# First image's sampling in turn with the other images' offsets, with TensorE and VectorE in a written order

## The chip, the cores and the metric

The program runs on one core of one Trainium2 chip. The metric is the device time of one execution in microseconds (us); lower is better. A program computes on five engines: TensorE (PE, matrix products; the loading of weights into it is shown apart as PEld), VectorE (DVE), ScalarE (ACT), GpSimd (POOL) and SyncE (SP). Each works through its own queue of instructions in order and waits on semaphores where it needs another's result. Transfers between the chip's main memory and its on-chip buffers are issued from the queues of SP, ACT or POOL and run on 16 DMA engines. Results of PE land in PSUM, a small memory of banks, from where VectorE or ScalarE must fetch them.

## The reference

Four images of 64 x 64 pixels with 256 channels go through a deformable convolution block, then through additive attention and a feed-forward layer that treats half of the tokens. Everything is in 32-bit floats. The change touches the first block alone, cut here to what matters:

```python
xp = x @ in_w + in_b                                   # projection, padded to 66 x 66
x1 = silu(bn(depthwise_conv3x3(x)))                    # x is group-normalised before
offset = x1 @ off_w + off_b                            # 8 groups x 9 taps x 2
mask = softmax((x1 @ mask_w + mask_b).reshape(N, H, W, G, P), -1)
...
loc = ref + grid * OFFSET_SCALE + offset * (OFFSET_SCALE / norm)
samples = _bilinear_sample(img, 2.0 * loc - 1.0)       # per group and tap, at moved positions
out = (samples * m).sum(-1)
...
return out @ out_w + out_b                             # x = x + this
```

Each output pixel is, for each of 8 groups of channels, a weighted sum of bilinear samples at nine moved positions. While an offset stays within one pixel, all samples of a pixel lie in a 5 x 5 window around it. The kernel therefore makes 25 weights per pixel and group and sums 25 shifted products; the few tokens with larger offsets are gathered exactly.

## The kernel before

Tokens of an image (4096) are taken in slabs. The first stage, `offsets_and_weights` (L263), goes through all four images before anything else. It works in slabs of `SLAB` = 8 rows of 128 tokens, so four slabs an image, with these inner functions:

- `front` (L322) loads the image in eight pieces `xt` (SP's queue, pool `a_ld` with three buffers), turns them on PE (L339), takes `bn_stats` on VectorE (L341), copies them to `xn` on ScalarE (L342), and normalises at the end (L349 to L366). It is a generator; the next image's pieces are fetched two per slab.
- `convolution` (L412) is the depthwise 3 x 3: half of the channels as nine matmuls with diagonal weights per 512 tokens (L420), the other half as nine VectorE instructions per slab (L432, L434); SiLU on ScalarE.
- `taps` (L437) makes offsets and masks with PE (L444), VectorE adds the bias into `raw` (L448), and the softmax begins (L456 to L458).
- `window` (L461) ends the softmax (L463 to L465), stores `raw`, makes three `hat` weights on ScalarE (L473 to L477), and builds the 5 x 5 weights `w5` with three `my` (L483), nine `mxy` (L486) and nine additions (L488) on VectorE. Then PE turns `w5` (L497), ScalarE copies it to `wT` and SP stores it in `wt`.
- `projection` (L380) computes `xp` for 16 rows of pixels with PE (L387), stores it, and turns it in nine pieces (L405), which ScalarE copies to `tb` (L406) and SP stores in the table `tab` that the exact gathers read (L407).

In this stage the order of the instructions on each engine is chosen by the scheduler of the tile framework. PSUM is split into four buffers for turns (`a_t`) and four for matmuls (`a_m`).

Between the stages, borders of `xp` and `tab` are filled with zeros (L1387 to L1397, SP's queue).

The second stage is `sample_image(0, 6)` (L668), a generator of some 440 steps (`STEPS`). It lists the tokens that need exact rows (`list_tokens`, L534), then goes over four blocks of 1024 tokens, two halves of channels and 25 window positions. A step is one product of the shifted image `xs` with a weight `wb` (L697), or one addition into `ac` (L705). `wb` is a 512 KB load, spread over partitions (L688). The argument `depth` = 6 gives `wb` twelve buffers and `xs`, `prd` and `ac` two. Between the steps `exact_rows` (L563) gathers the listed tokens' samples on POOL's queue (L626) and sums them on VectorE (L637, L640). At the end of a block the output matmuls follow (L721), POOL adds the bias to the input rows `xr` (L725), VectorE adds both (L728) and SP stores the rows (L729).

After that, image by image, come attention preparation, attention and feed-forward. The sampling of images 1 to 3 runs as steps within these later stages, with `depth` = 1, so with two `wb` buffers.

`keep` marks an instruction as staying in the written order relative to the other marked ones of its engine; `Pinned` (L254) wraps VectorE so that all its operations are marked.

Of the kernel before, what the change touches and what calls it, by code (L numbers as in the profile page):

```python
# [45 lines left out]
def layers_kernel(ctx: ExitStack, tc: tile.TileContext, a, out: bass.AP):  # L46
# [207 lines left out]
    class Pinned:  # L254


        def __getattr__(self, name):
            op = getattr(nc.vector, name)
            return lambda *args, **kw: keep(op(*args, **kw))  # L259

    pinned = Pinned()

    def offsets_and_weights(images, slab, rows_bufs):  # L263

        ca = S.a_one
# [52 lines left out]
        diag = ca.tile([P, K2, P], F32, name="diag")  # L318
        for tap in range(K2):
            nc.vector.tensor_scalar(diag[:, tap], ident, dwk[:, 1, tap : tap + 1], None, ALU.mult)  # L320

        def front(n):  # L322
# [8 lines left out]
            for s in range(8):  # L331
                xt = S.a_ld.tile([P, 4, C], F32, tag="xt", name="xt")
                nc.sync.dma_start(
                    out=xt, in_=x_d[n, s * 512 : (s + 1) * 512].rearrange("(t p) c -> p t c", p=P)
                )
                for k in range(CC):
                    pt = S.a_t.tile([P, 4, P], F32, tag="pt", name="pt")
                    for t in range(4):
                        nc.tensor.transpose(pt[:, t, :], xt[:, t, k * P : (k + 1) * P], ident)  # L339
                    ptf = pt.rearrange("p t q -> p (t q)")  # L340
                    nc.vector.bn_stats(st[:, k, s, :], ptf)  # L341
# [3 lines left out]
                    )  # L345
                yield
            mv = S.a_sm.tile([P, CC, 2], F32, tag="mv", name="mv")
            for k in range(CC):
                nc.vector.bn_aggr(mv[:, k, :], st[:, k].rearrange("p s f -> p (s f)"))  # L349
# [3 lines left out]
            nc.tensor.matmul(pg, gavgf, mv[:, :, 0], start=True, stop=True)  # L353
            gm = S.a_sm.tile([P, CC], F32, tag="gm", name="gm")
            nc.vector.tensor_copy(gm, pg)
            gv = S.a_sm.tile([P, CC], F32, tag="gv", name="gv")
            nc.vector.tensor_sub(gv, mv[:, :, 0], gm)
            nc.vector.tensor_mul(gv, gv, gv)
            nc.vector.tensor_add(gv, gv, mv[:, :, 1])
            pg2 = S.a_t.tile([P, CC], F32, tag="pt", name="pg2")  # L360
            nc.tensor.matmul(pg2, gavgf, gv, start=True, stop=True)
            gr = inv_std(S.a_sm, pg2, CC, "gr")
            nc.vector.scalar_tensor_tensor(gm, gm, -1.0, gr, ALU.mult, ALU.mult)
# [9 lines left out]
        for at, n in enumerate(images):  # L373
            xn = xns.pop(n)
            after = front(images[at + 1]) if at + 1 < len(images) else iter(())
# [4 lines left out]
            def projection(s):  # L380
                xp = xps[s % len(xps)]
                for h in range(2):
                    for f in range(CC):
                        pm = S.a_m.tile([P, 8, W], F32, tag="pm", name="pm")
                        r0 = 16 * s + 8 * h
                        for k in range(CC):
                            nc.tensor.matmul(  # L387
# [9 lines left out]
                for f in range(CC):  # L397
                    nc.sync.dma_start(out=xp_d[n][f][:, q0 : q0 + 16 * MP], in_=xp[:, f, : 16 * MP])
                for o in range(0, 16 * MP, P):
# [3 lines left out]
                    for c in range(2):  # L403
                        for f in range(CC):
                            nc.tensor.transpose(pt[:m, c, f, :], xp[:, f, o + c : o + c + m], ident)  # L405
                        nc.scalar.copy(tb[:m, :, :, c, :], pt[:m, c].rearrange("p f (e g) -> p f g e", g=GH))  # L406
                    nc.sync.dma_start(out=tabw[q0 + o : q0 + o + m], in_=tb[:m].rearrange("p f g c e -> p (f g c e)"))  # L407


            x1s, raws = {}, {}  # L410

            def convolution(s):  # L412
# [3 lines left out]
                for o in range(0, slab * P, 512):  # L416
                    pc = S.a_m.tile([P, 8, W], F32, tag="pm", name="pc")
                    for tap in range(K2):
                        r = r0 + o // W + tap // 3
                        nc.tensor.matmul(  # L420
                            pc, diag[:, tap], xn[:, 1, r : r + 8, tap % 3 : tap % 3 + W],
                            start=(tap == 0), stop=(tap == K2 - 1),
                        )
                    nc.scalar.activation(
                        x1[:, 1, o : o + 512], pc.rearrange("p r w -> p (r w)"), AF.Silu,
                        bias=bnsh[:, 1:2], scale=bns[:, 1:2],
                    )
                acc = x1[:, 0].rearrange("p (r w) -> p r w", w=W)
                for tap in range(K2):
                    src = xn[:, 0, r0 + tap // 3 : r0 + tap // 3 + 2 * slab, tap % 3 : tap % 3 + W]  # L430
                    if tap == 0:
# [73 lines left out]
            for s in range(ns):  # L505
                if s + 1 < ns:
                    convolution(s + 1)
# [970 lines left out]
```

## Time and profile before

| | |
|---|---|
| runs | 10553.36, 10569.91, 10557.95 us; median 10557.95 us |
| profiled execution | 10563.61 us, its span from first to last instruction 10561.9 us |
| mean granted TensorE clock | 0.917 |
| busy over the span | PE 9008.4 us (85%), VectorE 8547.2 (81%), ScalarE 7377.6 (70%), GpSimd 5265.2 (50%) |
| offsets of images 0, 1, 2, 3 | 190, 195, 196, 209 us, from 55 us on |
| sampling of image 0 | 845 to 1490 us |
| attention and feed-forward | 1490 us to the end |

The span is what the profiler sees of one execution; the time of a run has a little more around it. A line of a group names source line, engine, operation, written and read tiles, shape and count, then busy time and mean duration, then how long the engine stood idle just before these instructions and who ended that. A line of the timeline gives start, duration and, in square brackets, the idle time before. Durations of VectorE instructions that follow each other overlap by some 0.1 us, so the sum of durations is a little more than the busy time. A 32-bit matmul is recorded as two passes, so counts of matmuls are twice those in the source; transposes are one.

### The profile page before, as it was taken

The numbers are of one execution on the slowest core, as the hardware profiler recorded it, in microseconds if no ns is written. First come the engines' busy times: TensorE is split into PE (matmuls) and PEld (weight loads), VectorE is DVE, ScalarE is ACT, GpSimd is POOL, SyncE is SP. The second block draws the span as 40 slices with busy tenths as digits, with TensorE's granted clock in tenths as the row PEclk, the third lists the DMA queues.
The fourth block names the chain that finished last, engine by engine and source line by source line (L and its number), as shares of the span: only waits on it lengthen the run. The fifth ranks groups of instructions, "written<-read, shape, count | busy, mean of one in ns | idle before, by whom it ended". The sixth has DMA issues, their size and how long they took to land. (4 is left out here: it accounts for less than half of the span.)

```text
span 10561.9 us, 115936 instructions
## 1 busy us (share of the span) xinstructions
PE 9008.4 (85%) x38460; PEld 4375.8 (41%) x38460; DVE 8547.2 (81%) x13406; ACT 7377.6 (70%) x8389; POOL 5265.2 (50%) x3059
## 2 busy tenths in 40 slices
PE   7882029999999678999999589999999699999995
PEld 4551014444444343444444344444444344444443
DVE  7776879898989778989899679899898357777772
ACT  4450018888888528888888438888888379999991
POOL 0004307676555326767655327676555155555552
PEclk8985569999999889999999789999999799999997
DMA  3336752222222252212111352222111300000002
GB/s 119 107 138 180 206 167 70 61 67 64 70 64 73 98 167 60 52 55 58 51 55 50 116 152 53 53 54 54 52 59 41 101 13 9 10 8 7 7 5 75
DMA packets 381330, 766.00 MB, mean 73 GB/s; under 512 B 49105, under 2 KB 212593, under 8 KB 380689
## 3 DMA queue, kind: packets, MB, share of 16 engines
q1 hardware_dynamic: 324432, 678.78, 20.3%
q0 software_dynamic: 30144, 45.87, 2.9%
q10 hardware_dynamic: 26112, 33.56, 0.9%
q8 instruction: 309, 5.06, 0.2%
q14 instruction: 333, 2.72, 0.1%
HBM read 580.88 MB, written 177.14 MB: 72 GB/s over the span
## 5 line engine op out<-in xcount | busy, mean ns | idle before, releaser
L909 DVE TENSOR_TENSOR r<-nn,r 128x512 f32<-128x512 f32 x6144 | 3943.0, 683 | 861.5 <-PE nn L904 805.9
L904 PE MATMUL nn<-qn,kf 32*128 32x512 f32 (+1 forms) x12288 | 4518.8, 640 | 132.7 <-DVE r L909 95.8
L994 POOL TENSOR_TENSOR r<-r 128x1024 f32<-128x1024 f32 x1024 | 2708.8, 2645 | 2645.4 <-DVE r L909 2625.3
L988 ACT ACTIVATE r<-d 128x1024 f32<-128x1024 f32 x3072 | 3117.2, 1015 | 1085.4 <-DVE r L998 699.9
L894 PE MATMUL d<-qf,kf 32*128 32x512 f32 (+1 forms) x12288 | 3338.1, 632 | 76.5 <-DMA qf<-qf 43.1
L990 ACT ACTIVATE r<-r 128x1024 f32<-128x1024 f32 x3072 | 3124.1, 1051 | 32.6
L904 PEld LDWEIGHTS nn<-qn,kf 32*128 32x128 f32 (+1 forms) x12288 | 1399.4, 185 | 1902.1 <-DVE r L909 1450.5
L932 PE MATMUL pv<-v,et 128*128 128x257 f32 x8192 | 2105.3, 400 | 15.0 <-DVE acv L956 15.0
L932 PEld LDWEIGHTS pv<-v,et 128*128 128x128 f32 x8192 | 1507.6, 194 | 975.5 <-issue 768.6
L894 PEld LDWEIGHTS d<-qf,kf 32*128 32x128 f32 (+1 forms) x12288 | 1018.0, 186 | 1340.3 <-issue 736.1
L996 POOL TENSOR_TENSOR r<-r 128x512 f32<-128x512 f32 x1024 | 1335.8, 1304 | 92.7 <-DVE r L909 17.1
L705 DVE TENSOR_TENSOR ac<-ac,prd 128x1024 f32<-128x1024 f32 x768 | 991.8, 1291 | 8.8
L697 DVE TENSOR_TENSOR prd<-xs,wb 128x1024 f32<-128x1024 f32 x768 | 977.7, 1273 | 15.2 <-DMA wb<-wt 12.0
L626 POOL DMA_INDIRECT ga<-tab,tii x576 | 718.3, 1247 | 207.3 <-issue 117.7
L916 ACT ACTIVATE et<-et,nshift 128x512 f32<-128x512 f32 x1024 | 723.8, 707 | 28.2 <-DVE et L1001 28.2
L998 DVE TENSOR_TENSOR r<-r 128x512 f32<-128x512 f32 x1024 | 723.6, 707 | 4.1 <-POOL r L994 3.7
L1001 DVE TENSOR_TENSOR et<-r 128x512 f32<-128x512 f32 x1024 | 698.1, 682 | 0.4
L115 ACT ACT_TABLE_LOAD x9 | 11.5, 1283 | 799.3 <-DVE mv L259 703.0
L721 PE MATMUL pmo<-outwp,ac 128*128 128x256 f32 x512 | 135.7, 416 | 469.1 <-DVE ac L705 431.2
L480 POOL MEMSET w<- 128x1600 f32 x16 | 22.9, 1432 | 675.0 <-PE ptw L497 352.3
L721 PEld LDWEIGHTS pmo<-outwp,ac 128*128 128x128 f32 x512 | 100.8, 205 | 521.4 <-DVE ac L705 304.5
L420 PE MATMUL pc<-xn,diag 128*128 128x512 f32 x576 | 262.2, 609 | 33.4 <-ACT xn L366 33.4
(344 smaller groups left out, 5282.7 us busy)
## 6 DMA issues: line engine op xcount, KB each, us to landing
wb<-wt SPq DMA_DIRECT2D x800, 512.0 KB
tab<-tb SPq DMA_DIRECT2D x128, 256.0 KB
v<-t SPq DMA_DIRECT2D x64, 512.0 KB
xs<-xp SPq DMA_DIRECT2D x32, 680.0 KB
xp<-xp SPq DMA_DIRECT2D x32, 544.0 KB
xt<-in_x_dram SPq DMA_DIRECT2D x32, 512.0 KB
xr<-in_x_dram SPq DMA_DIRECT2D x64, 256.0 KB
t<-xr SPq DMA_DIRECT2D x64, 256.0 KB
```

Source lines behind the costliest of these rows:

```text
L697: keep(nc.vector.tensor_tensor(pr.rearrange("p (r w) -> p r w", w=W), src, wb.rearrange("p (r w) -> p r w", w=W), ALU.mult,))
L705: keep(nc.vector.tensor_add(ac[:, f, :], ac[:, f, :], pr))
L894: keep(nc.tensor.matmul(d[:, j, :], kf[g, blk, rows(kt)], qs[q][0][g, blk, :], start=True, stop=True))
L904: keep(nc.tensor.matmul(nn, kf[g, blk, rows(kt)], qs[q][1][g, blk, :], start=True, stop=True))
L909: keep(nc.vector.tensor_tensor(r[:, j, :], ns[j], r[:, j, :], ALU.mult))
L916: keep(nc.scalar.activation(ets[b], ets[b], AF.Exp, bias=nshift))
L932: keep(nc.tensor.matmul(pv, ets[b0 + i][:, rows(j)], v[:, k0 + i, :], start=(i == 0), stop=(i == PVB - 1)))
L988: keep(nc.scalar.activation(rs[b, p], ds.pop((b, p)), AF.Ln))
L990: keep(nc.scalar.activation(rs[b, p], rs[b, p], AF.Exp, scale=-1.0))
L994: keep(nc.gpsimd.tensor_tensor(rs[b, 1], rs[b, 1], rs[b, 2], ALU.add))
L996: keep(nc.gpsimd.tensor_tensor(rs[b, 1][:, 0], rs[b, 1][:, 0], rs[b, 3][:, 0], ALU.add))
L998: keep(nc.vector.tensor_add(rs[b, 1][:, 1], rs[b, 1][:, 1], rs[b, 3][:, 1]))
```

## The change

The first image's offsets stay a stage of their own. From the second image on, offsets and sampling of image 0 take turns, in an order written in the source: `offsets_and_weights` becomes a generator with five stops per slab, and the caller takes 4, 4, 4, 3 and 3 sampling steps at these stops. The slab is halved (`SLAB // 2`, eight slabs an image). All operations of TensorE and VectorE in this stage are marked by `keep`. The turning of `w5` becomes `turn`, one slab after its `window`; `convolution` is one slab ahead. In images 1 to 3 both halves of the channels of the depthwise convolution go to TensorE. Loads of `xt` move from SP's queue to POOL's, and stores of `xp`, `tab` and `wt` and the zero fill from SP's to ACT's; the zero fill moves ahead of the stage. Buffers: `a_ld` two instead of three, `wb` two instead of twelve, `xs` and `prd` one instead of two, `my` and `mxy` one instead of two, one `xps` instead of two, PSUM three `a_t`, three `a_m` and two for sampling.

```diff
-    pinned = Pinned()
+    pinned = Pinned(nc.vector)
...
+        vec, pe = pinned, Pinned(nc.tensor)
...
-        diag = ca.tile([P, K2, P], F32, name="diag")
-        for tap in range(K2):
-            nc.vector.tensor_scalar(diag[:, tap], ident, dwk[:, 1, tap : tap + 1], None, ALU.mult)
+        diag = ca.tile([P, CC, K2, P], F32, name="diag")
+        for k in (1, 0):
+            for tap in range(K2):
+                nc.vector.tensor_scalar(diag[:, k, tap], ident, dwk[:, k, tap : tap + 1], None, ALU.mult)
...
-                nc.sync.dma_start(
+                nc.gpsimd.dma_start(
                     out=xt, in_=x_d[n, s * 512 : (s + 1) * 512].rearrange("(t p) c -> p t c", p=P)
                 )
...
-                    nc.vector.bn_stats(st[:, k, s, :], ptf)
...
+                    ptfs.append(ptf)
+                yield
+                for k in range(CC):
+                    vec.bn_stats(st[:, k, s, :], ptfs[k])
                 yield
...
-                    nc.sync.dma_start(out=xp_d[n][f][:, q0 : q0 + 16 * MP], in_=xp[:, f, : 16 * MP])
+                    nc.scalar.dma_start(out=xp_d[n][f][:, q0 : q0 + 16 * MP], in_=xp[:, f, : 16 * MP])
...
+                for k in range(CC):
+                    if k == 0 and not at:
+                        acc = x1[:, 0].rearrange("p (r w) -> p r w", w=W)
...
+                        continue
+                    for o in range(0, slab * P, 512):
+                        pc = S.a_m.tile([P, 8, W], F32, tag="pm", name="pc")
+                        for tap in range(K2):
+                            r = r0 + o // W + tap // 3
+                            pe.matmul(
+                                pc, diag[:, k, tap], xn[:, k, r : r + 8, tap % 3 : tap % 3 + W],
+                                start=(tap == 0), stop=(tap == K2 - 1),
+                            )
...
+                vec.tensor_reduce(omax[:, n, s * slab : (s + 1) * slab], hat[:, 1], AX.X, ALU.max)
+                yield
...
                 for ey in range(3):
-                    my = S.a_w1p.tile([P, slab, GP], F32, tag="my", name="my", bufs=2)
+                    my = S.a_w1p.tile([P, slab, GP], F32, tag="my", name="my")
...
+                    yield
+
+            def turn(s):
...
-                        nc.sync.dma_start(out=wt_d[n][f, :, o : o + 512], in_=wT[: GH * ND])
-
-            ns = NT // slab
-            convolution(0)
-            for s in range(ns):
-                if s + 1 < ns:
-                    convolution(s + 1)
-                taps(s)
-                window(s)
-                for i in range(s * (H // 16) // ns, (s + 1) * (H // 16) // ns):
-                    projection(i)
-                for _ in range(8 // ns):
+                        nc.scalar.dma_start(out=wt_d[n][f, :, o : o + 512], in_=wT[: GH * ND])
...
+        for i in range(len(images) * ns):
+            at, s = divmod(i, ns)
+            if s == 0:
+                cur = ahead
+                after = front(images[at + 1]) if at + 1 < len(images) else iter(())
+            cur.taps(s)
+            if last:
+                last[0].turn(last[1])
+            last = cur, s
+            if s + 1 < ns:
+                cur.convolution(s + 1)
+            elif at + 1 < len(images):
+                ahead = image(at + 1)
+                ahead.convolution(0)
+            window = cur.window(s)
+            for part in range(4):
+
+                if part == 0 and s >= ns // 2 or part == 2 and s >= ns // 2 or s < ns // 2:
                     next(after, None)
-            for _ in after:
-                pass
+                if at:
+                    yield
+                next(window, None)
+            if at:
+                yield
+            for j in range(s * (H // 16) // ns, (s + 1) * (H // 16) // ns):
+                cur.projection(j)
+            if at == 0 and s == ns - 1:
+                yield
+        last[0].turn(last[1])
...
-    def sample_image(n, depth=1):
+    def sample_image(n, sums=1):
...
-            ac = S.dn.tile([P, CC, CH], F32, tag="ac", name="ac", bufs=min(depth, 2))
+            ac = S.dn.tile([P, CC, CH], F32, tag="ac", name="ac", bufs=sums)
...
-                    wb = S.dn.tile([P, CH], F32, tag="wb", name="wb", bufs=2 * depth)
+                    wb = S.dn.tile([P, CH], F32, tag="wb", name="wb", bufs=2)
...
-    with scope(
-        ("a_one", 1, 0), ("a_xn", 2, 0), ("a_ld", 3, 0), ("a_wk", 2, 0), ("a_w1p", 1, 0), ("a_sm", 2, 0),
-        ("a_t", 4, 1), ("a_m", 4, 1),
-    ):
-        offsets_and_weights(range(NB), SLAB, 2)
...
-    with scope(("smp", 2, 0), ("two", 2, 0), ("sb", 2, 0), ("dn", 1, 0), ("ps_m", 2, 1)):
-        for _ in sample_image(0, 6):
+    with scope(
+        ("a_one", 1, 0), ("a_xn", 2, 0), ("a_ld", 2, 0), ("a_wk", 2, 0), ("a_w1p", 1, 0), ("a_sm", 2, 0),
+        ("smp", 2, 0), ("two", 2, 0), ("sb", 2, 0), ("dn", 1, 0), ("a_t", 3, 1), ("a_m", 3, 1), ("ps_m", 2, 1),
+    ):
+        others = offsets_and_weights(range(NB), SLAB // 2, 1)
+        next(others)
+        first = sample_image(0, 2)
+        for at, _ in enumerate(others):
+            for _ in range((4, 4, 4, 3, 3)[at % 5]):
+                next(first, None)
+        for _ in first:
             pass
```

## The prediction

> **What bounds the kernel now.** I read first the busy tenths in 40 slices, to see which stages the change touches. The first six slices (264 us each) are the offsets of all images (a), then the sampling of image 0 (b); from the sixth on the attention runs, which the change does not touch.
>
> ```profile
> span 10561.9 us, 115936 instructions
> PE   7882029999999678999999589999999699999995
> DVE  7776879898989778989899679899898357777772
> PEclk8985569999999889999999789999999799999997
> DMA  3336752222222252212111352222111300000002
> ```
>
> Then the busy time by stretch, cut at the start of each image and at the end of sampling (columns: stretch, length, busy PE, PEld, DVE, ACT, POOL with counts, granted clock, DMA share, GB/s).
>
> ```profile
> 0.00:55.00 55.00, 17.11 (x80) 13.94 (x80) 39.31 (x138) 15.91 (x22) 18.77 (x52) 0.91 0.42 127
> 55.00:245.00 190.00, 158.23 (x612) 95.45 (x612) 138.36 (x184) 93.28 (x163) 6.79 (x12) 0.90 0.37 129
> ...
> 845.00:1490.00 645.00, 60.98 (x202) 48.57 (x202) 524.60 (x526) 0.00 (x0) 206.53 (x164) 0.53 0.65 193
> ```
>
> Stages a and b end one after the other at 1490 us, 14% of the span. An image costs 190 to 209 us, and neither engine is full: PE 158, VectorE 138, each stopping for the other. Sampling is VectorE alone: 525 of 645 us, with PE nearly idle at clock 0.53. Over the 1490 us VectorE is busy 1118. So 372 us are VectorE's idle time, and that is all that interleaving can win, apart from work taken off it.
>
> Third, the groups of the two stages (before 845, and 845 to 1500):
>
> ```profile
> L434 DVE SCALAR_TENSOR_TENSOR x<-xn,dwk,x 128x1024 f32<-128x1024 f32 x128 | 163.4, 1277 | 2.7
> L488 DVE TENSOR_TENSOR w<-w,mxy 128x576 f32<-128x576 f32 x144 | 108.3, 752 | 0.5
> L448 DVE TENSOR_TENSOR raw<-po,omb 128x432 f32<-128x432 f32 x64 | 37.7, 603 | 95.8 <-PE po L444 95.8
> L406 ACT COPY tb<-ptc 128x256 f32<-128x256 f32 (+1 forms) x288 | 98.1, 385 | 53.2 <-PE ptc L405 28.5 <-DMA tab<-tb 24.0
> ...
> L637 DVE TENSOR_TENSOR ga<-ga,wg 128x1152 f32<-128x1152 f32 x8 | 10.9, 1358 | 41.9 <-DMA ga<-tab,tii 41.9
> L728 DVE TENSOR_TENSOR xr<-pmo,xr 128x512 f32<-128x512 f32 x16 | 11.1, 692 | 43.7 <-POOL xr L725 29.8 <-PE pmo L721 13.3 <-PE pso L649 0.5
> ```
>
> The reader sees VectorE waiting 95.8 us for the offset matmuls in a, and some 86 us for gathers and for the output rows in b. Such waits can be filled by the other stage's work. Fourth, four stretches of the timeline that price the new waits:
>
> ```profile
> 230.49 8.27 SPq L407 DMA_DIRECT2D tab<-tb  x7
> 252.81 0.34 PEld L420 LDWEIGHTS pc<-xn,diag 128*128 128x128 f32 x1 [0.52 <-issue]
> 269.92 0.19 PEld L420 LDWEIGHTS pc<-xn,diag 128*128 128x128 f32 x1 [0.24 <-issue]
> 1478.70 2.48 POOL L725 TENSOR_TENSOR xr<-xr,outb 128x512 f32<-128x512 f32 x2 [118.85 <-DMA xr<-in_x_dram]
> ```
>
> **The change, part by part.** Image 0 keeps a stage of its own, now in 8 slabs. The other three images make 24 rounds of one slab (512 tokens), and each round takes 5 turns with 18 steps of sampling: 432 of its some 440.
>
> *VectorE per round.* An image costs 138 us, of which the depthwise taps (L432, L434) are 4 x (0.75 + 10.5) = 45; these go to PE in images 1 to 3, 136 us in all. The remaining 93 are done in half-size pieces. A 512-element instruction against a 1024-element one (0.68 against 1.22 us) gives 0.146 us + 1.047 ns an element, so 288 elements take 0.45, and 0.48 with the dependence on the one before, now that `mxy` has one buffer. The 21 window products take 10.1 us a slab; twice that is 5.5 more than now (21 x 0.70 = 14.7), and some 0.8 comes from the other small ones. That is 25 an image: 118 us, or 14.8 a round. Sampling adds 525 / 24 = 21.9. A round is 36.6 us, 24 are 879.
>
> *PE per round.* 18 depthwise matmuls of two passes at 0.43 us: 15.5; taps 3.0; turning the window weights 1.2 (38.3 us / 32); every second round a projection: 8 x 2 x 0.44 = 7.1 and 36 transposes. On average under 30 us, below VectorE. But both orders are fixed, and so the path matters: the turn waits for VectorE's last window product of the round before; behind it in PE's queue stand the convolution, the next image's transposes, the projection, and then the taps that VectorE's next round opens with. The projection's transposes are emptied through `tb`, which drops from three buffers to two: seven stores took 8.27 us, 1.18 each, so I take 1.18 x 3/2 = 1.77, or 16 us for nine. The path in a projection round: 1.2 + 15.5 + 2.6 (transposes, half of them) + 7.1 + 16 + 1.5 (first taps) = 41 to 44. VectorE covers it with 36.6 + 3.6 (three steps still follow the last window product) = 40.2. A cold clock is added: at 252.81, after PE had waited 8.4 us, weight loads came every 0.86 us instead of 0.43 for about 5.2 us, a loss of 2.6. In half of these rounds the transposes' PSUM buffers are held until VectorE's bn_stats late in the round, which leaves some 10.6 us of VectorE work against 15 of PE. So a projection round is 4 to 6 us late: 5 x 12 = 60. Bounds: 0 (stores land as now) and 138 (half of the convolution's passes cold: 11.5 x 12).
>
> [...]
>
> *Weight loads.* `wb` drops from twelve buffers to two. Between releasing a buffer and needing it again VectorE does two adds, a product and usually a window quarter: 1.14 + 1.25 + 1.14 + 3.4 = 6.9 us. The price of a load from the rows: the output rows `xr` (256 KB) were issued at 1473.9 and used at 1478.7, 4.8 us; twice the bytes at the 222 GB/s of the window 1200 to 1400 add 1.2, so 6.0 us. That fits, barely. Traffic per round is 102 MB / 32 + 127 MB / 24 = 8.5 MB, over 43 us 198 GB/s, like b now. I take 0.2 us a load, 40 us. Bounds: 3 us (over the whole run `wb` with two buffers in images 1 to 3 made VectorE wait 12.0 us in 18 places) and 260 (1.3 us a load, where steps stand four in a row).
>
> *Smaller waits in the rounds.* The output matmuls of three of the four blocks of rows stand ahead of the next taps: 28 passes took 8.56 us from 1467.5 on, at clock 0.53; warm (half of 0.43 for half the columns) some 6, and 1.5 for the first taps, 7.5 x 3 = 22 (0 to 30). Listing the tokens and fetching their offsets: 15 (0 to 25). `xs` with one buffer: 1.5 x 7 = 10 (0 to 35). The 41.9 us for the gathers go: ten products then last 40 us, 18 gathers 22.7 (18 x 1.26).
>
> *Image 0.* VectorE needs 118 + 8 x (0.41 + 8 x 0.71) = 167, without sampling to cover PE. In four of eight rounds PE's path is 1.2 + 7.7 + 7.1 + 16 + 1.5 = 33.5 against 20.9: 12.6 x 4 = 50. So 215 for now 190 (180 to 245).
>
> *Before and after.* The loads of `xt` move to POOL's queue, with two buffers: 55 becomes 60 (55 to 80, from 0.95 us, the shortest L626, to 5.0, four of them, for each of 8 issues). Stores on ACT's queue are taken at nothing: ACT is busy 97 of 195 us an image, and a round's 7 issues at some 0.4 us (SP's) hide in that; without cover 24 x 3 = 72. The zero fill at 845 also leaves the path. At the end remain the last output rows, 20 us, as now 23.
>
> *Sum.* 60 + 215 + (879 + 60 + 22 + 15 + 40 + 10 = 1026) + 20 = 1321 for 1490: 169 us less. The profiled execution took 10563.6 us (span 10561.9), so 10395; it lies 6 us above the median of the runs, 10557.95, and so the forecast is **10390 us**. With the terms apart, 10280 to 10500.
>
> **The rivals.**
> *VectorE alone sets the rounds (0.15).* PE runs far enough ahead and loads land in time: 55 + 180 + 879 + 37 + 3 + 20 = 1174 (smaller waits 22 + 15, loads 3), 316 less, 10240. For it: PE's 30 us a round are under 36.6. Against it: the projection path of 41 to 44 us.
> *PE's path sets the projection rounds (0.13).* Half of the convolution runs cold: 60 + 235 + 879 + 138 + 47 + 40 + 20 = 1419, 71 less, 10490. For it: the granted clock was 0.77 in stretches where PE was busy 70% (700 to 860). Against it: a run of 15 us of convolution outlasts the 5.2 us of the cold start.
> *The two weight buffers decide (slower, 0.09).* If a `wb` load needs 9 us from release to landing, because stores of `tb`, `xp` and `raw` go on the same DMA engines, VectorE stops 2.1 us in each of 200 loads: 1321 - 40 + 420 = 1701, 211 more, 10770. It decides from 7.9 us on ((1490 - 1281) / 200 = 1.05 over 6.9). For it: b moved 193 GB/s with twelve loads in flight, not two. Against it: the 6.0 us estimated, and that a late VectorE also leaves more time for the next load.
> *The change doesn't do what it says.* In the changed program's instruction order products of sampling and of windows alternate on VectorE from image 1 on, so I leave this out.
>
> **How the numbers follow.** The forecast has 0.63, the rivals 0.15, 0.13 and 0.09. A measurement of this kernel can't tell less than 0.2% (21 us) from no change. Slower: 0.09 and 0.01 from the end of PE's case; within 0.2%: 0.03, the same end; faster: 0.87. The range 10280 to 10500 leaves out most of the first rival and all of the third.
>
> **What would show it.** Attention should start near 1320 us instead of 1490. Right: VectorE busy over 85% of the rounds, some 41 to 43 us apart; its waits, in this order, for `po` (some 110 us with image 0) and for `wb` (under 100); depthwise matmuls x1008 instead of x576, and no taps on VectorE after image 0. Wrong: rounds over 50 us (then `wb` or `tb` heads the waits), image 0 over 245 us, or ACT late in its own queue because a store waits there.

## The result, and the profile after

| | before | changed |
|---|---|---|
| median of the runs, us | 10560.17 (10553.36 to 10573.17) | 10625.76 (10600.88 to 10638.48) |
| ratio to before | | 1.006, 95% interval 1.0049 to 1.007 |
| span of the profiled execution, us | 10561.9 | 10621.5 |
| attention begins (its first `bn_stats`), us | 1498.4 | 1554.0 |

The changed kernel is 0.6% slower; 10390 us was forecast. The start of attention moved by 55.6 us and the span by 59.6, so nearly all of the loss lies in the stages that the change rewrites.

The page of the changed kernel, busy tenths in 40 slices of 266 us:

```profile
span 10621.5 us, 117482 instructions
...
PE   5766659999999778999999589999999699999995
...
DVE  5677778899999778989899679999898457777772
...
PEclk8777779999999879999999789999999799999997
DMA  3455543222212242212111252212111200000002
```

Before, PE went from 8 in the offsets to 2 and 0 in the sampling. Now it stands at 5 to 7 in all of the first six slices, and VectorE at 5 to 7 too: the two stages did mix, but neither engine fills up. The granted clock stays at 7 in five of these slices.

The stretches of the changed kernel, cut behind the first half of the first normalisation, at the first sampling product and at the end of sampling (columns as in the prediction):

```profile
0.00:104.70 104.70, 20.02 (x80) 15.75 (x80) 39.18 (x147) 16.44 (x23) 24.03 (x62) 0.89 0.31 94
104.70:392.00 287.30, 211.55 (x698) 130.93 (x698) 179.59 (x383) 121.42 (x193) 12.95 (x23) 0.79 0.26 87
392.00:1520.00 1128.00, 741.98 (x2290) 423.14 (x2288) 851.71 (x1202) 343.07 (x574) 207.60 (x205) 0.78 0.55 168
1520.00:1554.00 34.00, 22.42 (x83) 19.83 (x83) 13.45 (x49) 1.28 (x1) 3.69 (x4) 0.60 0.56 181
```

In the 24 rounds (third line) VectorE has 852 us of work and takes 1128, 47 a round. TensorE has 742, at clock 0.78. VectorE stands idle for a quarter of the time, TensorE for a third. Set against the sum that was forecast (the first normalisation begins at 100.9, the last sum into `ac` ends at 1520.7):

| term | forecast, us | measured, us |
|---|---|---|
| up to the first normalisation | 60 | 100.9 |
| image 0 alone | 215 | 291.1 |
| 24 rounds | 1026 | 1128.7 |
| rest, to attention | 20 | 33.3 |
| sum | 1321 | 1554.0 |

The groups that answer to those shown of before, over the first 1554 us:

```profile
L262 DVE TENSOR_TENSOR w<-w,mxy 128x288 f32<-128x288 f32 x288 | 132.1, 459 | 11.5
L262 DVE BATCH_NORM_STATS2 st<-pt 128x6 f32<-128x512 f32 x64 | 42.0, 689 | 86.2 <-ACT xn L351 68.6 <-issue 17.4
L262 DVE TENSOR_TENSOR raw<-po,omb 128x432 f32<-128x432 f32 x64 | 37.2, 602 | 187.4 <-PE po L262 177.6 <-issue 6.9 <-PE ptw L262 3.0
L782 DVE TENSOR_TENSOR xr<-pmo,xr 128x512 f32<-128x512 f32 x16 | 11.1, 691 | 39.8 <-PE pmo L775 22.3 <-POOL xr L779 17.5
L691 DVE TENSOR_TENSOR ga<-ga,wg 128x1152 f32<-128x1152 f32 x8 | 10.8, 1351 | 0.0
...
L425 ACT COPY tb<-ptc 128x256 f32<-128x256 f32 (+1 forms) x288 | 105.6, 371 | 259.9 <-PE ptc L262 127.0 <-DMA tab<-tb 118.2 <-remote 5.4
```

The wait that the interleaving should have filled, `raw` for the offset matmuls `po`, grew from 95.8 us to 187.4. A second one stands beside it: `bn_stats` waits 86.2 us, where before it was 55.5:

```profile
L341 DVE BATCH_NORM_STATS2 st<-pt 128x6 f32<-128x512 f32 x64 | 43.0, 692 | 55.5 <-PE pt L339 55.4
```

(VectorE's depthwise line is gone after image 0. `bn_stats` and ScalarE's copy to `xn` read the same tile, so the releaser `xn` is read here as the turned piece `pt` of PE that both need.) Only the gathers' wait went as meant, from 41.9 to 0.0. ScalarE's copies to `tb` now wait 118.2 us for the stores of `tab` that still hold their buffer, 24.0 before.

Where this happens is seen in one round. The timeline of TensorE, 437 to 494 us (start, length, instruction, idle time before):

```profile
437.22 1.92 PE L262 MATMUL ptw<-ident,w 128*100 128x128 f32 x8 [10.34 <-DVE w L262]
438.93 16.70 PE L262 MATMUL pc<-xn,diag 128*128 128x512 f32 x36
455.46 1.47 PE L262 MATMUL pt<-ident,xt 128*128 128x128 f32 x12
...
468.10 0.44 PE L262 MATMUL ptc<-ident,xp 128*128 128x128 f32 x2 [0.46 <-ACT tb L425]
469.01 0.69 PE L262 MATMUL ptc<-ident,xp 128*128 128x128 f32 x2 [0.46 <-ACT tb L425]
...
483.31 1.11 PE L262 MATMUL ptc<-ident,xp 128*128 128x128 f32 x4 [4.00 <-issue]
...
488.86 4.78 PE L262 MATMUL po<-wom,x 128*128 128x216 f32 x16
```

and VectorE in the same stretch:

```profile
456.95 1.30 DVE L262 BATCH_NORM_STATS2 st<-pt 128x6 f32<-128x512 f32 x2 [7.40 <-ACT xn L351]
...
491.99 0.61 DVE L262 TENSOR_TENSOR raw<-po,omb 128x432 f32<-128x432 f32 x1 [5.76 <-issue]
495.60 0.61 DVE L262 TENSOR_TENSOR raw<-po,omb 128x432 f32<-128x432 f32 x1 [3.00 <-PE ptw L262]
```

TensorE waits 10.3 us for VectorE's last window product, then goes through its blocks as they are written: the turn, 16.7 us of convolution, the next image's pieces, the projection, its turned pieces from 465.1 to 488.9, the taps. VectorE stops 7.4 us at `bn_stats`, because the piece stands behind the convolution, and 8.8 at `raw`, because the taps stand behind all of it (both `raw` wait for `po`; "issue" and `ptw` are what the profile saw last). So in one round each engine waits for the other. From the turn to VectorE's first addition into `raw` (437.22 to 491.99) it is 54.8 us, where the forecast had 41 to 44 for this path.

### The profile page after: what moved, and what is told of

It is laid out like the page before. It is cut to its first block, busy times and chain, and to the rows that moved or that the text cites. A ratio compares the mean times of both kernels' runs of the same rounds, so it can differ in the third digit from the quotient of the medians.

```text
span 10621.5 us, 117482 instructions
## 1 busy us (share of the span) xinstructions
PE 9295.3 (88%) x38892; PEld 4520.2 (43%) x38892; DVE 8506.3 (80%) x13775; ACT 7467.1 (70%) x8525; POOL 5258.6 (50%) x3106
## 3 DMA queue, kind: packets, MB, share of 16 engines
q1 hardware_dynamic: 273552, 592.06, 17.3%
## 5 line engine op out<-in xcount | busy, mean ns | idle before, releaser
L680 POOL DMA_INDIRECT ga<-tab,tii x576 | 689.8, 1198 | 274.8 <-DVE so L694 125.9
L262 PE MATMUL pc<-xn,diag 128*128 128x512 f32 x1008 | 461.3, 617 | 8.3 <-ACT xn L383 8.3
L506 POOL MEMSET w<- 128x800 f32 x32 | 25.2, 787 | 710.4 <-PE ptw L262 694.5
L262 PE MATMUL ptc<-ident,xp 128*128 128x128 f32 (+1 forms) x576 | 148.9, 395 | 225.4 <-ACT tb L425 209.7
L262 PEld LDWEIGHTS pc<-xn,diag 128*128 128x128 f32 x1008 | 198.2, 200 | 249.9 <-issue 238.7
L425 ACT COPY tb<-ptc 128x256 f32<-128x256 f32 (+1 forms) x288 | 105.6, 371 | 259.9 <-PE ptc L262 127.0
```

## The experiments

Ratios are to the kernel before on the same chip. Its median was 10528 us for the first twelve kernels and 10564 us for the last three (`h1`, `h3`, `h4`); the changed kernel's own ratio is 1.006.

### Buffers, the zero fill and the place of the turn

`e1_zero`: the zero tile as a small constant outside a pool of its own.

```diff
-    with scope(("one", 1, 0)):
-        zm = S.one.tile([P, 2 * G * 2 * CG], F32, name="zm")
+    if True:
+        zm = const.tile([P, 256], F32, name="zm")
...
+                tabz = tabw[q0 : q0 + 2 * MP].rearrange("(p r) (h c) -> p (r h) c", r=2, h=2)
...
-                    out=tabw[q0 : q0 + 2 * MP].rearrange("(p r) c -> p (r c)", r=2), in_=zm[:MP]
+                    out=tabz, in_=zm[:MP].rearrange("p (o c) -> p o c", o=1).to_broadcast([MP, 4, 256])
```

> The zero fill's source tile is 1 KB in the constants' pool instead of 4 KB in a pool of its own that is closed before the stage opens; the same bytes are stored. Theory (the stage's tiles lie where the fill's source lay, so the constants' loads wait 40 us for the fill's stores): the constants are loaded at 27 us instead of 63, the first normalisation of image 0 ends near 65 instead of 105 us, and the time falls by 35 to 45 us, to some 10583. Rival (the DMA engines are simply busy with the fill, and the loads would queue behind it): the loads land late anyway, and less than 10 us are won.

Measured: 10553.26 us, 1.0026 (1.0015 to 1.0038). The first normalisation begins at 77.6 us instead of 100.9, attention at 1514.2 instead of 1554.0. The timeline of the changed kernel shows what was removed; `zm` lay in memory that the next stage's tiles reuse, and these wait until the fill's last store has read it:

```profile
54.85 1.98 ACTq L1444 DMA_DIRECT2D tab<-zm  x1
...
63.01 0.20 POOL L313 MEMSET gavg<- 128x128 f32 x1 [35.52 <-DMA tab<-zm]
...
66.65 0.56 PE L281 MATMUL pb<-inb,perm 128*128 128x2 f32 x2 [40.58 <-DMA wom<-in_L_conv_mask_w_dram]
```

In `e1_zero` neither of the two waits, 35.5 and 40.6 us, is listed. So the fill, which the forecast took off the path, costs about 36 us (1.006 - 1.0026 of 10560) at its new place. At its old place VectorE had waited for it twice before the first product, by the view of waits of the kernel before (in all, times, longest):

```profile
DVE fl L542 <- DMA xp<-zm: 19.6, 1, 19.6
DVE fl L542 <- DMA tab<-zm: 15.9, 1, 15.9
```

That is 35.5 us too, so by these numbers the move won nothing. The fill is not all of the prologue's excess: 77.6 is still 25.9 over the 51.7 of before. In this run ScalarE's first copies to `xn` stand 24.8 us behind the fill's stores on its queue.

`e2_turn` writes the turn of slab s-1 behind the convolution of slab s+1; `e8_end` writes it at the end of the round, behind the projection.

```diff
             cur.taps(s)
-            if last:
-                last[0].turn(last[1])
-            last = cur, s
...
                 ahead.convolution(0)
+            if last:
+                last[0].turn(last[1])
+            last = cur, s
```

> The turning of the window weights of the slab before stands behind the convolution on TensorE instead of ahead of it; nothing else. Theory (TensorE stands at the turn until VectorE's last window product, 160 us in all, and convolution, transposes and projection queue behind it, so VectorE then waits for taps and bn_stats, 187 us in the rounds): these waits of VectorE fall by more than half, the rounds from 47 to 41 to 43 us, and the time by 80 to 160 us, to 10465 to 10545. Rival (the projection's turning, 25 us through two buffers, sets the rounds by itself): less than 40 us.

> The turn of the slab before stands at the end of the round, behind the projection, on TensorE; otherwise as the changed kernel. If the wait at the turn is the cause, this is at least as good as the turn behind the convolution (80 us less, ratio 0.998): 80 to 140 us less, ratio 0.993 to 0.998, with TensorE's wait at the turn near nothing. If the two turn tiles at the end get into the way of the next projection or ScalarE's order, it is 0 to 60 us less.

Measured: `e2_turn` 10509.22 us, 0.9981 (0.997 to 0.9991); `e8_end` 10498.09 us, 0.9967 (0.9955 to 0.9978). TensorE's wait for VectorE's window product in the rounds falls from 139.8 us (and 21.5 in one more stop, which the profile puts to `mxy`) to 36.5 and 20.3. VectorE's wait for `po` there falls less, from 106.5 to 71.4 and 66.7, and TensorE's wait for `tb` rises from 176.6 to 212.4 and 201.2. The early turn was one of several stops in the chain of blocks; with it gone the next stop takes over.

`e3_tb3` gives `tb` a third buffer (and `st` one instead of two, for room).

```diff
-                    tb = S.a_ld.tile([P, CC, GH, 2, CG], F32, tag="tb", name="tb")
+                    tb = S.a_ld.tile([P, CC, GH, 2, CG], F32, tag="tb", name="tb", bufs=3)
...
-            st = S.a_sm.tile([P, CC, 8, 6], F32, tag="st", name="st")
+            st = S.a_sm.tile([P, CC, 8, 6], F32, tag="st", name="st", bufs=1)
```

> Three buffers for the projection's turned pieces instead of two (and one for the statistics of the next image instead of two, for room). Theory that the path through these stores sets the projection rounds: a projection's turning falls from some 25 to 17 us, in 16 projections 128 us of the path, and the time by 60 to 130 us. Theory that TensorE's early turn sets them: the path is shorter by the same, but only the part past VectorE's cover counts, 30 to 80 us. Rival (TensorE's low clock and ScalarE's copies set the 25 us, not the stores): less than 15 us.

Measured: 10499.36 us, 0.9976 (0.9966 to 0.9985): 0.0084 or 89 us less than the changed kernel. TensorE's wait for `tb` falls to 125.2 us, VectorE's for `po` to 58.4, but its `bn_stats` still wait 56.2 and the turn 165.1.

`f2_psum` gives the turns four PSUM buffers and the sampling one.

```diff
-        ("smp", 2, 0), ("two", 2, 0), ("sb", 2, 0), ("dn", 1, 0), ("a_t", 3, 1), ("a_m", 3, 1), ("ps_m", 2, 1),
+        ("smp", 2, 0), ("two", 2, 0), ("sb", 2, 0), ("dn", 1, 0), ("a_t", 4, 1), ("a_m", 3, 1), ("ps_m", 1, 1),
```

> Four PSUM tiles for turns and one for sampling, instead of three and two; nothing else. Theory (in half of the projection rounds the next image's transposes hold two of the three turn tiles until VectorE's bn_stats, so TensorE and ScalarE take turns over the one that is left, 0.9 us a copy): those projections take some 5 us less, in 7 or 8 of 16, and the time falls by 20 to 50 us, ratio 1.001 to 1.004. Rival (the stores through two buffers set the pace there too): less than 10 us, ratio 1.005 to 1.007. With one PSUM tile for sampling the listing and the output rows may get some 10 us slower.

Measured: 10573.03 us, 1.004 (1.0026 to 1.0054), overlapping the changed kernel's own interval. It lies at the edge of what was expected if PSUM held the turns up, and the sampling lost a buffer for it. So a gain of some 20 us isn't ruled out, but PSUM for the turns is not what makes the rounds long.

`f1_comb` takes the small zero tile, the turn behind the convolution and the third `tb` together (for room, `st` with one buffer and the weights `inw` loaded into a tile of `xt`).

> Together: the zero fill's tile out of the way, the turn behind the convolution, three buffers for the projection's turned pieces (room from loading one weight through the image pieces' tile). Singly they took about 40, 80 and 90 us off the changed kernel. If turn and stores lengthen the same path in different places (theory), most adds up: 160 to 210 us less, ratio to the kernel before 0.986 to 0.991. If both only take away the same wait, as either makes the path shorter than VectorE's cover: 120 to 140 us less, ratio about 0.994.

Measured: 10412.95 us, 0.9892 (0.9875 to 0.9908). The single gains against 1.006 are 0.0034, 0.0079 and 0.0084, together 0.0197; the sum is 0.0168. They mostly add, and VectorE's wait for `po` in the rounds falls to 17.3 us.

### TensorE's written order

`e6_pefree` changes one line: TensorE's instructions are no longer marked, so the scheduler places them. VectorE keeps its written order.

```diff
-        vec, pe = pinned, Pinned(nc.tensor)
+        vec, pe = pinned, nc.tensor
```

> TensorE's operations in the stage are not held to the written order, VectorE's are; nothing else. If the written order on TensorE is what makes it wait at the turn (theory), the scheduler is free to put convolution and projection ahead of it, and the time falls by 40 to 120 us, ratio 0.994 to 1.002. If the scheduler takes nearly the same order, or the waits come from buffers: within 20 us of the changed kernel, ratio 1.004 to 1.008.

Measured: 10356.65 us, 0.983 (0.9814 to 0.9846), some 240 us less than the changed kernel and twice the most that was expected. The order of TensorE's instructions in the free kernel, from its timeline:

```profile
819.80 0.38 PE L424 MATMUL ptc<-ident,xp 128*128 128x128 f32 x2
820.02 1.02 PE L452 MATMUL pc<-xn,diag 128*128 128x512 f32 x2
820.88 0.38 PE L424 MATMUL ptc<-ident,xp 128*128 128x128 f32 x2
821.10 1.02 PE L452 MATMUL pc<-xn,diag 128*128 128x512 f32 x2
...
830.89 0.44 PE L424 MATMUL ptc<-ident,xp 128*128 128x128 f32 x2 [0.50 <-ACT tb L425]
831.17 1.03 PE L775 MATMUL pmo<-outwp,ac 128*128 128x256 f32 x4
832.03 0.53 PE L468 MATMUL po<-wom,x 128*128 128x216 f32 x2
```

A pair of transposes (half of a turned piece), one convolution matmul (two passes), another pair: while ScalarE copies a pair to `tb` and the store of `tab` runs, TensorE works on the convolution, and the taps begin before the last pieces. The stretches of this kernel, prologue, image 0 and rounds (the first normalisation begins at 102.7):

```profile
0.00:104.70 104.70, 23.56 (x92) 18.81 (x92) 39.31 (x147) 15.23 (x23) 24.78 (x63) 0.85 0.32 94
104.70:363.10 258.40, 222.66 (x810) 131.77 (x811) 180.86 (x386) 131.75 (x212) 13.36 (x24) 0.91 0.31 104
363.10:1297.00 933.90, 682.09 (x2165) 366.22 (x2163) 849.48 (x1198) 324.62 (x551) 209.59 (x203) 0.88 0.65 202
```

VectorE has the same 849 us of work in the rounds and takes 934 instead of 1128: busy 91%. Neither `po` nor `bn_stats` stands among its waits there; first come two for transfers, then the output rows, by the view of waits:

```profile
DVE prd L751 <- DMA wb<-wt: 14.4, 12, 4.1
DVE ac L751 <- DMA xs<-xp: 11.1, 3, 5.7
DVE xr L782 <- PE pmo L775: 8.7, 5, 3.4
```

Was the move of the convolution to TensorE itself a mistake? `e5_dveconv` and `g2_freeconv` put its second half back on VectorE in all images, the one with TensorE's order written, the other with it free.

```diff
-                    if k == 0 and not at:
+                    if k == 0:
```

> In all images half of the channels of the depthwise convolution on VectorE, as in image 0 and in the kernel before. VectorE gets 24 x 5.3 = 127 us more, TensorE 186 us less. If TensorE's path sets the rounds: its path is 7.7 us shorter in each, so 24 x 5.3 more work and some 100 to 150 us less waiting: within 30 us of the changed kernel's 10626. If VectorE's work sets the rounds: 100 to 130 us longer, some 10740. If TensorE's sheer load at a clock of 0.78 sets them: faster by 30 us or more.

> TensorE's order free and the second half of the convolution back on VectorE in all images. If the move to TensorE was right and only the written order spoiled it, VectorE (near 90% busy in the rounds of the free run) pays most of the 136 us that come back to it: 100 to 136 us over the free run, a ratio of 0.993 to 0.996. If TensorE is the limit there too, no loss: 0.980 to 0.984.

Measured: 1.0047 (1.003 to 1.0064, 10582.88 us) and 0.997 (0.9957 to 0.9982, 10501.96 us). The rounds of the two, first with the written order, then free:

```profile
384.40:1516.50 1132.10, 594.49 (x1874) 366.84 (x1874) 995.31 (x1409) 342.59 (x572) 210.50 (x205) 0.70 0.54 168
```

```profile
358.80:1421.30 1062.50, 561.28 (x1783) 334.07 (x1781) 986.49 (x1396) 333.88 (x556) 209.34 (x203) 0.73 0.58 177
```

| rounds, us (VectorE busy) | TensorE in written order | free |
|---|---|---|
| half of the convolution on VectorE | 1132 (995) | 1063 (986) |
| all on TensorE (images 1 to 3) | 1128 (852) | 934 (849) |

This table holds the case. With the written order, 144 us less work on VectorE shortens the rounds by 4 us: VectorE's work is not what sets them. (The work went to TensorE, whose busy time rises by 147 us, so this pair alone doesn't tell its load from its order.) With the free order 137 us less shorten them by 129, though TensorE takes on the same work. `g2_freeconv` cost a little more over the free run (0.014) than the 0.010 to 0.013 expected.

The two runs in the upper line also part the order from the clock. Their granted clocks in the rounds are 0.70 and 0.73, both below the changed kernel's 0.78. Yet VectorE waits 54.9 us for `po` in the written order, and in the free one neither `po` nor `bn_stats` is listed and the rounds are 70 us shorter. So these waits are gone at a granted clock of 0.73 too.

Which part of the written order does it? `g3_tposefree` frees all transposes and keeps the matmuls; `h4_mmfree` is its complement, with the matmuls of projection, convolution and taps free. `h1_convfree` frees the convolution alone, `h3_tapsfree` the taps alone. One line of each kind of edit:

```diff
-                            pe.transpose(pt[:m, c, f, :], xp[:, f, o + c : o + c + m], ident)
+                            nc.tensor.transpose(pt[:m, c, f, :], xp[:, f, o + c : o + c + m], ident)
...
-                            pe.matmul(
+                            nc.tensor.matmul(
```

> TensorE's matmuls keep their written order, all its transposes (of the loaded image, of xp, of the window weights) are left to the scheduler. If what stands in the way are the turned pieces that wait for tb, for the last window product and for bn_stats, this brings nearly all that the free order brought: 0.983 to 0.988 of the kernel before. If it is the order of the matmul blocks themselves (convolution ahead of the taps), little: 1.000 to 1.006. In between, both take part.

> The complement of the run with free transposes: all matmuls free, all transposes kept among themselves. In the compiled order pairs of turned pieces alternate with single convolution matmuls, as in the fully free run. If this interleaving is what the free order brings, 0.983 to 0.988; if both kinds must be free together, 0.993 or more.

> Only the convolution's matmuls are left to the scheduler, all else on TensorE keeps its written order. If the 15.5 us block of the convolution ahead of the turned pieces and the taps is what VectorE waits for, most of what the free order brought comes back: 0.985 to 0.992. If a single block's freedom doesn't help because the taps still stand behind the projection's pieces, 1.000 to 1.006.

> Only the offset matmuls of the taps are left to the scheduler; in the compiled order they now stand among the projection's turned pieces (after 2 to 6 of 36) instead of behind them. If VectorE's wait for po behind those pieces is the main loss, the wait for po (106.5 us in the rounds of the changed kernel) falls below 40 us and the ratio is 0.990 to 0.996. If the rounds are set by TensorE's total path, the time moves to another wait: 1.000 to 1.006.

| | us | ratio, interval | VectorE in the rounds waits for `po`, for `bn_stats` | TensorE for `tb`, for `w` |
|---|---|---|---|---|
| none free (changed kernel) | 10625.76 | 1.006 (1.0049 to 1.007) | 106.5, 70.4 | 176.6, 139.8 |
| transposes free | 10555.83 | 1.0023 (1.0013 to 1.0032) | 102.3, 52.0 | 155.5, 167.6 |
| convolution free | 10535.25 | 0.9974 (0.9964 to 0.9984) | 48.9, 33.0 | 185.3, 38.9 |
| taps free | 10524.14 | 0.996 (0.9946 to 0.9974) | not listed, 74.0 | 145.5, 116.9 |
| all matmuls free | 10394.51 | 0.9835 (0.9818 to 0.9851) | not listed, not listed | 73.6, 64.5 |

Free transposes bring little, 0.0037: the matmuls keep their blocks, and hardly anything is left to put between the pieces. One free group removes one wait and meets the next: with free taps VectorE no longer waits for `po`, and in its place stand

```profile
DVE st L262 <- ACT xn L351: 57.1, 6, 19.0
DVE xr L782 <- PE pmo L775: 38.6, 5, 22.7
DVE omax L262 <- ACT hat L499: 19.5, 7, 5.4
```

With all matmuls free and the transposes in their written order among themselves, the whole gain of the free order is there (0.9835 and 0.983, intervals overlapping). The order of TensorE's instructions shows the same pattern, pairs of transposes and single convolution matmuls in turn:

```profile
815.45 0.38 PE L262 MATMUL ptc<-ident,xp 128*128 128x128 f32 x2
815.67 1.02 PE L452 MATMUL pc<-xn,diag 128*128 128x512 f32 x2
```

So it is the freedom of the matmuls that counts, not the order of the turned pieces: that theory (0.983 to 0.988) missed. The convolution alone came out at 0.9974, between the two ranges expected. The taps alone did what was expected if the wait for `po` is the main loss: that wait went, and 0.996 is the end of the range (0.990 to 0.996). But against 1.006 the taps give 0.010 and the convolution 0.0086, and all matmuls 0.0225, so neither is the whole cause. The projection's matmuls alone, and pairs of groups, were not run, so it is not shown whether the shares of the groups simply add up or need each other. That blocks leave nothing to fill the stops is read from the timelines. ScalarE's instructions and the transfers are placed by the scheduler in all these runs, and what their order did was not held apart.

### Both kernels beaten

`g1_freecomb` is the free order with the small zero tile and the third `tb` (`st` and `inw` as in `f1_comb`); `g4_freelate` also writes the turn behind the convolution.

> The run with TensorE's order left to the scheduler (0.983 of the kernel before), and in it the small zero tile, three tb and one st. If the zero fill and TensorE's order are separate costs, the first normalisation comes at about 78 us instead of 103 and the 25 to 40 us are kept to the end: 0.979 to 0.981. If the third tb still matters where the scheduler may put other matmuls between the turned pieces (TensorE waited 90.6 us for tb in the rounds there), some 20 to 40 us more: 0.975 to 0.978. If the free order already covers both, 0.982 to 0.984.

> As the combined free run, with the turn written behind the next convolution. If the scheduler's free order already moves the turn out of the way, within 0.2% of that run; if the written place still sets the order of ScalarE's copies and stores, up to 0.5% either way.

Measured: 10342.2 us, 0.9812 (0.9796 to 0.9829), and 10325.59 us, 0.9801 (0.9785 to 0.9818): some 2% faster than the kernel before. The intervals of the two overlap, so the written place of the turn is worth nothing that can be told here. `g1_freecomb` lies between the ranges expected for two separate costs and for none, and its interval overlaps that of the free order alone. Its trace tells more: the first normalisation begins at 76.3 us instead of 102.7, and attention at 1303.6 instead of 1330.0. So the small zero tile gives 26 us, which are kept, and the third `tb` nothing beside it. TensorE's wait for `tb` between 392 and 1300 us falls from 90.6 to 41.4 us and its wait for `w` rises from 61.6 to 82.0, with VectorE busy for 91% either way.

## Why the prediction was wrong

*The direction.* Faster was forecast with 0.87; it was slower. The rival on the slower side, two `wb` buffers, was not what did it: VectorE waited 9.2 us for `wb` in the rounds, of 40 forecast and 260 feared, and 14.4 in the free order, where the rounds are shorter than forecast.

*VectorE per round.* Right: 879 us of work were forecast and 852 measured. The half-size products take 0.459 us, forecast 0.45 to 0.48. That all depthwise work leaves VectorE after image 0 was right too, and so was its size: 136 us forecast, 144 by the two runs with the written order.

*TensorE per round: the step that failed.* "VectorE covers it with 36.6 + 3.6 ... So a projection round is 4 to 6 us late: 5 x 12 = 60." The waits for `po` and `bn_stats` in the rounds together took 106.5 + 53.0 + 17.4 = 177 us. Three things in it were wrong:

- The turned pieces were priced by the pace of seven store issues on SP's queue (1.18 us each, times 3/2), 16 us; they took 23.8 in the round shown. Only part of that is the stores: ScalarE's copies waited for them in three places, 7.3 us in all. Up to 474 us TensorE and ScalarE take turns, a pair of transposes, then its copy, 0.9 to 1.15 us each time. The price held neither this turn-taking nor the granted clock of 0.50 that stands from 469 us on. That two `tb` cost time is shown by the third one, 89 us. The offsets matmuls behind them took 4.8 us for sixteen passes, where 1.5 was taken for the first half of them.
- `bn_stats` was not priced as a wait at all. That the next image's pieces stand behind the convolution on TensorE was written down, but only for what they delay on TensorE, and not for what VectorE, in a fixed order too, has queued behind `bn_stats`.
- The sum compared a path on TensorE with work on VectorE as though both began together. The turn begins when VectorE's last window product ends, and TensorE waited 139.8 us in the rounds for that (161.3 with the stop put to `mxy`). With both orders fixed the waits of the two engines follow each other and add up; the larger of two busy times is only a lower bound.

The rival "PE's path sets the projection rounds" named the right path, but its price was another, half of the convolution at a cold clock, and 10490 was too low. The convolution's passes took 610 ns on average in the rounds, against 609 before, with a median of 592 in both. In the round shown the granted clock is 0.50 from the start of the convolution (438.9 us) to 441 and 1.00 from there to its end at 455.6, so far less than half of it was cold.

*Image 0.* Forecast 215, measured 291 us. Of this VectorE was busy 180, and it waited 71.1 for `po`, where 50 was forecast, and 10.6 + 7.1 us for the listing, which had been put into the rounds. The free order brings it to 260 (363.1 - 102.7), still over the forecast: this part of the stage stays costlier than eight half slabs were taken to be, and what holds the rest was not followed up.

*Before.* "The zero fill at 845 also leaves the path": it left that place, where VectorE had waited 35.5 us for it in two places, and made a wait of 35.5 us on GpSimd's `gavg` and 40.6 us on TensorE's `pb` in the prologue. The move was costed as a step removed, and its issues and its memory were not followed to where they went. The moved `xt` loads, priced at 5 us, were small beside this: TensorE waited for them 8.4 us in five places between 78 and 94 us.

*After.* 33 us against 20. The last output rows take 16 us of it (1520.7 to 1536.6), then VectorE lists the next image's tokens until attention begins. Before, it was 31 us from the last sum to attention (1467.5 to 1498.4), so this part hardly changed; the 23 us that the forecast started from ended at 1490.

*Small waits.* Output rows 19.9 us for PE (forecast 22) and 9.4 more for GpSimd, which the forecast did not list; `xs` 9.5 (10), gathers 0 (0): close. The 28 output passes of before that priced the 22 us ran at a granted clock of 0.73 over their 8.56 us (1467.50 to 1476.06), not at 0.53.

*What would have shown it.* "Wrong: ... image 0 over 245 us" came true; rounds of 47.0 us stood between the bounds given (41 to 43, over 50). `po` did head VectorE's waits as forecast, at 177.6 us with image 0 where some 110 was given, but `bn_stats` stood second, which was not on the list. The free order's rounds of 38.9 us show that the work itself fitted into less than the forecast's 41 to 43.

## What to carry to other kernels

When two stages are interleaved with the order written out on two engines, follow the waits around the loop: for every instruction that waits, name what stands behind it on its own engine, and let the delay travel on to the other. In this kernel an order written in blocks that were efficient alone left no small piece of independent work to fill the stops; fix the order on the engine that should be full, and leave the one that has slack to the scheduler, or interleave its groups piece by piece. A test that costs little is to take work off the engine that is thought to be the limit: if the time stays, as here (4 us for 144), that engine's work is not the limit. Whether it is the other engine's load or the order, freeing the order tells.

## What the runs showed of the hardware

The clock fell in a stretch where TensorE never stood idle for long. In the round shown the granted clock is 1.00 from 465.1 to 467 us, 0.85 from there to 469, and 0.50 from 469 to 488.8. A pair of transposes takes 0.44 us up to 468.10 and 0.69 from 469.01 on. From 465.1 to 469.0 TensorE was busy for 1.70 of 3.90 us, and no gap was over 0.82 us. So here the clock fell to half without a long gap. What brings it down, no run here shows.

Over the rounds the granted clock was 0.78 in the written order and 0.88 in the free one. TensorE's 742 and 682 busy us there are not for the same work, as the free order did 125 recorded passes more ahead of the rounds. Over prologue, image 0 and rounds together the work is the same (3068 and 3067 passes), and TensorE is busy 974 and 928 us. From these figures I estimate that the warmer clock took some 45 us off its busy time, while the whole stretch is 223 us shorter; how much of the 45 lay on the path was not separated.
